# Expert tiles of layer 1: weight copies ahead of the row loads, smaller first units, and matmuls that keep TensorE occupied

## The chip, the cores and the metric

The kernel runs on one core of a Trainium2 chip. A core has five engines with instruction streams of their own: PE (TensorE, matmuls into PSUM), DVE (VectorE), ACT (ScalarE), POOL (GpSimd) and SP (SyncE, which here only issues DMAs). Each engine takes its instructions in order; between engines, order is kept by semaphores. The metric is the device time of one execution in microseconds (us), and a time of a kernel is the median over its runs.

## The reference

Two layers run one after the other over the same tokens, 8 sequences of 512 tokens with 128 channels. Each layer is an attention block (a recurrent scan) and a mixture of experts, both added to the residual. The change lies in the experts of layer 1:

```python
logits = hidden_states @ router_w + router_b
probs = jax.nn.softmax(logits, axis=-1)
topw, topi = jax.lax.top_k(probs, K)                    # K = 4 of E = 16 experts
topw = topw / jnp.sum(topw, axis=-1, keepdims=True)
combine = jnp.sum(jax.nn.one_hot(topi, E) * topw[..., None], axis=2)

def body(acc, expert):
    w1e, b1e, w2e, b2e, ce = expert                     # 128 x 256, 256, 256 x 128, 128
    hmid = jax.nn.gelu(x @ w1e + b1e, approximate=False)
    return (acc + (hmid @ w2e + b2e) * ce[:, None], None)
```

So of 4096 tokens each goes to 4 of 16 experts: 16384 rows of work, each through two matmuls of 128 x 256 with a Gelu between them.

## The kernel before

**Stages.** The program runs layer 0's attention, layer 0's experts, layer 1's attention with its router, then layer 1's experts. Each stage has its own pools of tiles on the chip; a pool that opens where an older one was closed takes over its addresses, and then the first write of a new tile waits for the last use of whatever lay there.

**Layer 1's router** (`route1`) ends each sequence by scattering its rows: for each token tile and each of its four experts, POOL issues one indirect DMA (line 1532, 128 of them) that writes 128 rows of 130 numbers (128 channels, the weight of the expert, and the row's place in the result) into a table in memory, `rows1`, which has one region per expert. The order of this stage is found by a small planner (`Order`), which hands out engines by estimated costs and ranks.

**Layer 1's experts** (from line 1584) are written out by hand, in the order given. Rows of one expert are cut into tiles of 128; since how many rows an expert gets is known only at run time, there are 144 tiles, enough for the worst case, in 36 quads of four.

- `plan()` (lines 1619 to 1677) counts the rows of each expert and works out, for every tile, its expert, where its rows start in `rows1`, and which rows are to be dropped. A last pair of passes, line 1672, spreads one of these lists over the partitions.
- `fetch(q)` loads the four row tiles of a quad into `de` (line 1690): three from SP's queue, one from ACT's. Four quads are asked for ahead. All these loads wait until the last row scatter has landed.
- `prepare(q)` transposes the four tiles on PE (line 1696). For each tile DVE copies the weights of its expert out of the resident tables `fw1` and `fw2` at an offset read from `off1` (lines 1680, 1701, 1702), and then the transposed rows out of PSUM (`dT`, line 1703).
- `first(q)` multiplies by the first weights (line 1712, eight matmuls of 128 x 128) and ACT applies Gelu with its bias (line 1718, eight activations).
- `second(q)` multiplies by the second weights (line 1729, eight matmuls). DVE works out the destinations (`to`, line 1736) and scales the results (`qy`, line 1737). POOL then scatters them, one indirect DMA for each tile (line 1739, 144 in all), into `res1`.
- `results(b)` at the end loads the four results of each token back (`yk`), and POOL and DVE add them to the residual (lines 1775 and 1777).

The loop calls `prepare(q + 1)`, `first(q)`, `fetch(q + 4)` and `second(q - 1)` in this order for each `q`, after one `prepare(0)` ahead of it. Buffers: the weight copies `qw1` and `qw2` have three and four, `dT` and `qh` three, `y` four; the PSUM banks `qT` and `qyp` are two each and `mid` four.

The pool of all these tiles, `work2`, opens where layer 1's attention had its `work1`, in which the row scatters' sources (`rows`) lie as well.

`fill` (line 952) is an older piece: the planner may put matmuls of `ident` by `zeros` into gaps of PE in the earlier stages. None is in the expert stage.

Of the kernel before, what the change touches and what calls it, by code (L numbers as in the profile page):

```python
# [9 lines left out]
F32 = mybir.dt.float32  # L10
I32 = mybir.dt.int32
# [3 lines left out]
ALU = mybir.AluOpType  # L15
AX = mybir.AxisListType

P = 128
B = 8
S = 512  # L20
NT = S // P
C = 128
# [167 lines left out]
def two_layers(ctx: ExitStack, tc: tile.TileContext, a: dict, out: bass.AP):  # L190
    nc = tc.nc

    const = ctx.enter_context(tc.tile_pool(name="const", bufs=1))
# [31 lines left out]
    ident = const.tile([P, P], F32, name="ident")  # L225
# [212 lines left out]
    def tiled(t2):  # L438
        return t2.rearrange("p (t c) -> p t c", t=NT)
# [593 lines left out]
        nc.scalar.preload_act_table_set(EXP)  # L1033

    stage.close()
    work = stage.enter_context(tc.tile_pool(name="work1", bufs=1))
    small = stage.enter_context(tc.tile_pool(name="small1", bufs=1))

# [2 lines left out]
    full = [P, NT, K1, E1]  # L1041
    ys_ring = ring(work, 2, [P, NT, 2, C], "ys")
    u_ring = ring(work, 4, tokens, "u")
    hn_ring = ring(work, 2, tokens, "hn")
    h1_ring = ring(work, 2, columns, "h1T")
    v_ring = ring(work, 3, columns, "vT")
    gk_ring = ring(work, 2, [ng, S], "gk")
    kq_ring = ring(work, 2, columns, "kq")
    za_ring = ring(work, 2, [ng, S], "za")
    gate_ring = ring(work, 3, columns, "gate")  # L1050

    four = [P, DK, S]
    kb_ring = ring(work, 3, four, "kb")
# [531 lines left out]
    fw1, fw2 = late  # L1585

    stage.close()
    work = ctx.enter_context(tc.tile_pool(name="work2", bufs=2))


    de_ring = ring_of(work, 8, [P, 4, W1], "de")
    to_ring = ring_of(work, 4, [P, 4], "to", I32)
    w1_ring = ring_of(work, 3, [P, 4, WE], "qw1")
    w2_ring = ring_of(work, 4, [P, 4, I1], "qw2")
    dT_ring = ring_of(work, 3, [P, S], "dT")
    hT_ring = ring_of(work, 3, [P, NC1, S], "qh")
    y_ring = ring_of(work, 4, [P, 4, C], "qy")
# [94 lines left out]
    def prepare(q):  # L1692

        ps = qT_banks[q % 2]
        for i in range(4):
            nc.tensor.transpose(ps[:, i * P : (i + 1) * P], de[q][:, i, 0:C], ident)  # L1696
        w1_q, w2_q, dT = w1_ring[q % 3], w2_ring[q % 4], dT_ring[q % 3]
        for i in range(4):
            n = 4 * q + i
            at = value(off1[0:1, n : n + 1], ET.DVE, 0, (E1 - 1) * WE)  # L1700
            nc.vector.tensor_copy(w1_q[:, i, :], fw1[:, bass.ds(at, WE)])  # L1701
            nc.vector.tensor_copy(w2_q[:, i, :], fw2[:, bass.ds(at, I1)])  # L1702
        nc.vector.tensor_copy(dT, ps)  # L1703

    def first(q):

        w1_q, dT, hT = w1_ring[q % 3], dT_ring[q % 3], hT_ring[q % 3]
        mid = mid_banks[2 * (q % 2) : 2 * (q % 2) + 2]
        for i in range(4):
            here = slice(i * P, (i + 1) * P)  # L1710
            for c in range(NC1):
                nc.tensor.matmul(  # L1712
                    mid[c][:, here], lhsT=w1_q[:, i, c * P : (c + 1) * P], rhs=dT[:, here], start=True, stop=True
                )
        for i in range(4):
# [6 lines left out]
    def second(q):  # L1722

        w2_q, hT, to, y = w2_ring[q % 4], hT_ring[q % 3], to_ring[q % 4], y_ring[q % 4]
        ps = qy_banks[q % 2]
        for i in range(4):
# [9 lines left out]
        nc.vector.tensor_tensor(to, de[q][:, :, DEST].bitcast(I32), nowhere[:, 4 * q : 4 * q + 4], ALU.max)  # L1736
        nc.vector.tensor_mul(y, tiled(ps), de[q][:, :, WEIGHT : WEIGHT + 1].to_broadcast([P, 4, C]))
        for i in range(4):
            nc.gpsimd.indirect_dma_start(  # L1739
                out=res1_w[4 * q + i],  # L1740
                out_offset=bass.IndirectOffsetOnAxis(ap=to[:, i : i + 1], axis=0),
                in_=y[:, i, :],
                in_offset=None,
                bounds_check=NA - 1,
                oob_is_err=False,
            )
# [71 lines left out]
```

## Time and profile before

| what | us |
|---|---|
| median of six runs | 1025.02 (1018.0 to 1028.74) |
| the profiled execution, whole time | 1025.66 |
| its span on the core | 1023.9 |
| PE busy, of the span | 794.2 |
| DVE busy | 629.3 |
| ACT busy | 472.6 |
| POOL busy | 467.2 |
| last row scatter of the router (line 1532) starts | 780.90 |
| first result scatter (line 1739) starts | 798.28 |
| last result scatter starts | 985.05 |

The span is counted from the first instruction on the core; the whole time has 1.76 us more around it. A row of the timeline gives the start, the duration, the engine, the line in the kernel, the operation, output and inputs, how many such instructions are merged, and in brackets how long the engine stood idle before it and what released it. A group's row gives the busy time, then the mean duration of one in nanoseconds, then the idle time before the group. PE's operations are f32 matmuls here, and the trace records each pass of one. The granted clock of PE is 1.0 or 0.5 of the full one, in steps of 3.41 us.

### The profile page before, as it was taken

What the parts mean: (1) busy time and instruction counts of PE and PEld (TensorE: products, weight loads), DVE (VectorE), ACT (ScalarE), POOL (GpSimd) and SP (SyncE); (2) the same over time, 40 slices, a digit from 0 to 9 for tenths busy, and PEclk for the clock granted to TensorE, in tenths of its full rate; (3) what the DMA queues carried; (4) which work ended last, traced back from release to release, by engine and by line L of the source; (5) the groups of instructions that cost most, each with busy time, mean ns of one, the idle gap of its engine ahead of it and who ended that gap; (6) DMA issues with size and microseconds to landing.
All of it is one profiled execution on the core that took longest, in us unless ns stands there. A gap on an engine that the chain in (4) does not pass through costs nothing. (4 is left out here: it accounts for less than half of the span.)

```text
span 1023.9 us, 13443 instructions
## 1 busy us (share of the span) xinstructions
PE 794.2 (78%) x3819; PEld 520.9 (51%) x3819; DVE 629.3 (61%) x1584; ACT 472.6 (46%) x1040; POOL 467.2 (46%) x474
## 2 busy tenths in 40 slices
PE   5978999899798939969678899787942998988400
PEld 3635466455363614423346555455621997877400
DVE  5496999788767301114678666767552777666317
ACT  6543665663352414418545686465620553434200
POOL 6200003232844434530000826878774677777753
PEclk9896789898787759989988997978865999999855
DMA  7994675566244330026992406765212443332138
GB/s 177 219 266 109 164 185 141 148 169 141 68 111 112 107 84 12 16 83 180 231 229 73 120 14 155 193 186 161 91 50 71 126 116 105 98 100 78 50 132 280
DMA packets 81675, 131.93 MB, mean 129 GB/s; under 512 B 13044, under 2 KB 58998, under 8 KB 74432
## 3 DMA queue, kind: packets, MB, share of 16 engines
q1 hardware_dynamic: 52544, 91.12, 34.9%
q0 software_dynamic: 14832, 27.84, 9.3%
q10 hardware_dynamic: 14224, 12.11, 3.9%
q8 instruction: 30, 0.49, 0.2%
q14 instruction: 45, 0.37, 0.1%
HBM read 94.79 MB, written 41.14 MB: 133 GB/s over the span
## 5 line engine op out<-in xcount | busy, mean ns | idle before, releaser
L1532 POOL DMA_INDIRECT rows<-rows,si x128 | 152.5, 1191 | 175.1 <-DVE tmp L1502 113.6
L876 POOL DMA_INDIRECT row<-rows,si x64 | 90.2, 1409 | 212.6 <-DVE qT L587 109.0
L1739 POOL DMA_INDIRECT res<-qy,to x144 | 143.7, 998 | 60.4 <-issue 31.2
L1718 ACT ACTIVATE qh<-mid,qw 128x128 f32<-128x128 f32 x288 | 79.3, 378 | 121.6 <-PE mid L1712 86.6
L1712 PE MATMUL mid<-dT,qw 128*128 128x128 f32 x576 | 75.1, 286 | 18.8 <-DVE dT L1703 18.8
L671 PE MATMUL acc<-add,center 128*128 128x512 f32 x128 | 78.4, 770 | 9.7 <-DVE add L700 8.0
L1712 PEld LDWEIGHTS mid<-dT,qw 128*128 128x128 f32 x576 | 70.0, 199 | 23.4 <-DVE dT L1703 23.2
L694 DVE TENSOR_TENSOR_SCAN add<-dec,add 128x2048 f32<-128x2048 f32 x16 | 70.8, 4425 | 0.7
L1729 PE MATMUL qyp<-qw,qh 128*128 128x128 f32 x576 | 70.0, 275 | 0.0
L1729 PEld LDWEIGHTS qyp<-qw,qh 128*128 128x128 f32 x576 | 67.2, 192 | 0.0
L179 ACT ACT_TABLE_LOAD x48 | 61.6, 1283 | 5.4 <-issue 3.5
L1701 DVE COPY qw<-fw 128x258 f32 x144 | 45.0, 313 | 29.8 <-DMA rows<-rows,si 16.6
L671 PEld LDWEIGHTS acc<-add,center 128*128 128x128 f32 x128 | 30.9, 252 | 54.5 <-issue 35.7
L1012 POOL DMA_INDIRECT res<-y,de x32 | 31.4, 982 | 45.3 <-DVE dT L985 20.7
L789 PE MATMUL bank<-xT,rw 128*128 128x512 f32 x64 | 41.7, 787 | 5.5 <-ACT xT L781 3.8
L1702 DVE COPY qw<-fw 128x256 f32 x144 | 43.7, 303 | 0.2 <-issue 0.2
L1317 PE MATMUL acc<-ident,kb 128*128 128x128 f32 x256 | 36.2, 309 | 9.2 <-DVE kb L1307 9.2
L1317 PEld LDWEIGHTS acc<-ident,kb 128*128 128x128 f32 x256 | 34.9, 223 | 13.1 <-DVE kb L1307 13.0
L1777 DVE TENSOR_TENSOR x<-x,yk 128x512 f32<-128x512 f32 x24 | 24.1, 1012 | 28.5 <-DMA yk<-res 27.4
L952 PE MATMUL idle_bank<-zeros,ident 128*128 128x512 f32 x76 | 40.6, 662 | 0.8 <-DVE y L1006 0.8
L662 ACT ACTIVATE dec<-dec 128x2048 f32<-128x2048 f32 x16 | 30.5, 1908 | 22.6 <-DVE dec L682 22.6
L1696 PE MATMUL qT<-ident,de 128*128 128x128 f32 x144 | 23.4, 282 | 21.2 <-DMA de<-rows 21.1
(337 smaller groups left out, 1757.5 us busy)
## 6 DMA issues: line engine op xcount, KB each, us to landing
add<-keys SPq DMA_DIRECT2D x16, 1024.0 KB
qb_first<-queries SPq DMA_DIRECT2D x8, 1024.0 KB
qb_second<-queries SPq DMA_DIRECT2D x8, 1024.0 KB
kb<-pairs SPq DMA_DIRECT2D x8, 1024.0 KB
gb_both<-decays SPq DMA_DIRECT2D x8, 1024.0 KB
qb_both<-pairs SPq DMA_DIRECT2D x8, 1024.0 KB
yk<-res SPq DMA_DIRECT2D x8, 1024.0 KB
de<-rows SPq DMA_DIRECT2D x108, 65.0 KB
```

The costliest lines, as they stand in the source:

```text
L179: self.load(table)
L671: nc.tensor.matmul(acc, lhsT=center, rhs=st[:, j, :], start=g + j == 0, stop=(g + 1) * J + j == D + J - 1)
L694: nc.vector.tensor_tensor_scan(flat, dec.rearrange("p j t -> p (j t)"), flat, 0.0, ALU.mult, ALU.add)
L876: nc.gpsimd.indirect_dma_start(out=row0_w[(b * NT + t) * 2 + k], out_offset=bass.IndirectOffsetOnAxis(ap=m.si[:, t, k : k + 1], axis=0), i ...
L1317: nc.tensor.matmul(chunk(acc, t), lhsT=chunk(st[:, j, :], t), rhs=ident, start=j + t == 0, stop=j + t == DK + NT - 2)
L1532: nc.gpsimd.indirect_dma_start(out=rows1_w[(b * NT + t) * K1 + k], out_offset=bass.IndirectOffsetOnAxis(ap=m.si[:, t, k : k + 1], axis=0), ...
L1701: nc.vector.tensor_copy(w1_q[:, i, :], fw1[:, bass.ds(at, WE)])
L1702: nc.vector.tensor_copy(w2_q[:, i, :], fw2[:, bass.ds(at, I1)])
L1712: nc.tensor.matmul(mid[c][:, here], lhsT=w1_q[:, i, c * P : (c + 1) * P], rhs=dT[:, here], start=True, stop=True)
L1718: nc.scalar.activation(hT[:, c, here], mid[c][:, here], AF.Gelu, bias=w1_q[:, i, I1 + c : I1 + c + 1])
L1729: nc.tensor.matmul(ps[:, here], lhsT=hT[:, c, here], rhs=w2_q[:, i, c * C : (c + 1) * C], start=c == 0, stop=c == NC1 - 1,)
L1739: nc.gpsimd.indirect_dma_start(out=res1_w[4 * q + i], out_offset=bass.IndirectOffsetOnAxis(ap=to[:, i : i + 1], axis=0), in_=y[:, i, :], i ...
```

## The change

Four things are done together.

- The tiles of layer 1's attention are split over two pools, `early1` and `work1`. The weight rings `qw1` and `qw2` of the expert stage get a pool of their own, `early2`, which takes the place of `early1`; the tiles with the row scatters' sources stay in `work1`, under `work2`.
- The weight copies leave `prepare` for a function `weights(q)`. It is called for quads 0, 1 and 2 right after `plan()`, before any row is fetched, and for the others two quads ahead.
- The loop runs over units. Quad 0 is four units of one tile, quad 1 two units of two tiles, all others one unit of four tiles. `dT`, `qh`, `to`, `y` and the PSUM banks rotate by unit, the weights by quad.
- After the weight copies, `warm(24)` puts 24 matmuls of `ident` by `zeros` (128 x 512) on PE, then one matmul of one column on a tile `gate` that POOL sets to zero, then five more.

```diff
     stage.close()
+    early_work = stage.enter_context(tc.tile_pool(name="early1", bufs=1))
     work = stage.enter_context(tc.tile_pool(name="work1", bufs=1))
...
-    hn_ring = ring(work, 2, tokens, "hn")
+    hn_ring = ring(early_work, 2, tokens, "hn")
...
     stage.close()
+    early_work = ctx.enter_context(tc.tile_pool(name="early2", bufs=1))
     work = ctx.enter_context(tc.tile_pool(name="work2", bufs=2))
...
-    w1_ring = ring_of(work, 3, [P, 4, WE], "qw1")
-    w2_ring = ring_of(work, 4, [P, 4, I1], "qw2")
+    w1_ring = ring_of(early_work, 3, [P, 4, WE], "qw1")
+    w2_ring = ring_of(early_work, 4, [P, 4, I1], "qw2")
...
+    def weights(q):
+
+        w1_q, w2_q = w1_ring[q % 3], w2_ring[q % 4]
         for i in range(4):
             n = 4 * q + i
             at = value(off1[0:1, n : n + 1], ET.DVE, 0, (E1 - 1) * WE)
             nc.vector.tensor_copy(w1_q[:, i, :], fw1[:, bass.ds(at, WE)])
             nc.vector.tensor_copy(w2_q[:, i, :], fw2[:, bass.ds(at, I1)])
...
+    units = [(0, range(i, i + 1)) for i in range(4)] + [(1, range(0, 2)), (1, range(2, 4))]
+    units += [(q, range(4)) for q in range(2, QUADS)]
...
+    def prepare(u):
+
+        q, tiles_of = units[u]
+        ps, dT = qT_banks[u % 2], dT_ring[u % 3]
+        for i in tiles_of:
+            nc.tensor.transpose(ps[:, i * P : (i + 1) * P], de[q][:, i, 0:C], ident)
+        nc.vector.tensor_copy(dT[:, span(tiles_of)], ps[:, span(tiles_of)])
...
+    def warm(n):
+
+        for _ in range(n):
+            nc.tensor.matmul(mid_banks[3], lhsT=ident, rhs=zeros, start=True, stop=True)
+
     AHEAD = 4
+    gate = const.tile([P, 1], F32, name="gate")
     with tc.manual_schedule():
         plan()
+        for q in range(3):
+            weights(q)
+        warm(24)
+        nc.gpsimd.memset(gate, 0.0)
+        nc.tensor.matmul(mid_banks[3][:, 0:1], lhsT=ident, rhs=gate, start=True, stop=True)
+        warm(5)
         for q in range(AHEAD):
             fetch(q)
-        prepare(0)
-        for q in range(QUADS + 1):
-            if q + 1 < QUADS:
-                prepare(q + 1)
-            if q < QUADS:
-                first(q)
-            if q + AHEAD < QUADS:
-                fetch(q + AHEAD)
-            if q > 0:
-                second(q - 1)
+        for u in range(len(units) + 1):
+            here = u < len(units)
+            q = units[u][0] if here else QUADS
+            if u < 5:
+                prepare(u)
+            if 4 < u + 1 < len(units) and u >= 4:
+                prepare(u + 1)
+            if here:
+                first(u)
+                if units[u][1][0] == 0 and q + AHEAD < QUADS:
+                    fetch(q + AHEAD)
+            if u > 0:
+                second(u - 1)
+            if here and units[u][1][-1] == 3 and 0 < q < QUADS - 2:
+                weights(q + 2)
```

The rings `h1T`, `vT`, `gk`, `kq`, `za` and `kb` move to `early1` like `hn`. `first` and `second` do for the tiles of a unit what they did for the four of a quad: the matmuls, activations, destinations, multiplies and scatters are the same in number for each tile, and DVE's `dT`, `to` and `qy` are one instruction for each unit.

More of the change, by code (lines that the diff above doesn't have):

```diff
@@ L1043, in two_layers @@
     u_ring = ring(work, 4, tokens, "u")
-    hn_ring = ring(work, 2, tokens, "hn")
[L1045 to L1049, printed above, removed]
+    hn_ring = ring(early_work, 2, tokens, "hn")
+    h1_ring = ring(early_work, 2, columns, "h1T")
+    v_ring = ring(early_work, 3, columns, "vT")
+    gk_ring = ring(early_work, 2, [ng, S], "gk")
+    kq_ring = ring(early_work, 2, columns, "kq")
+    za_ring = ring(early_work, 2, [ng, S], "za")
     gate_ring = ring(work, 3, columns, "gate")
     four = [P, DK, S]
-    kb_ring = ring(work, 3, four, "kb")
+    kb_ring = ring(early_work, 3, four, "kb")
     gb_both = experts.tile([P, 2, DK, S], F32, tag="first", name="gb_both")
@@ L1690, in fetch @@
                 queue.dma_start(de[q][:, i, :], rows1[bass.ds(at[i - tiles_of[0]], P), :])
[L1692 to L1697, printed above, removed]
+    def weights(q):
+        w1_q, w2_q = w1_ring[q % 3], w2_ring[q % 4]
         for i in range(4):
@@ L1702, in prepare, with span, first @@
             nc.vector.tensor_copy(w2_q[:, i, :], fw2[:, bass.ds(at, I1)])
[L1703 to L1709, printed above, removed]
+    units = [(0, range(i, i + 1)) for i in range(4)] + [(1, range(0, 2)), (1, range(2, 4))]
+    units += [(q, range(4)) for q in range(2, QUADS)]
+    def span(tiles_of):
+        return slice(tiles_of[0] * P, (tiles_of[-1] + 1) * P)
+    def prepare(u):
[4 more added lines that the diff above has]
+        nc.vector.tensor_copy(dT[:, span(tiles_of)], ps[:, span(tiles_of)])
+    def first(u):
+        q, tiles_of = units[u]
+        w1_q, dT, hT = w1_ring[q % 3], dT_ring[u % 3], hT_ring[u % 3]
+        mid = mid_banks[2 * (u % 2) : 2 * (u % 2) + 2]
+        for i in tiles_of:
             here = slice(i * P, (i + 1) * P)
@@ L1714, in first @@
                 )
-        for i in range(4):
+        for i in tiles_of:
             here = slice(i * P, (i + 1) * P)
@@ L1720, in first, with second @@
                 )
[L1722 to L1726, printed above, removed]
+    def second(u):
+        q, tiles_of = units[u]
+        w2_q, hT, to, y = w2_ring[q % 4], hT_ring[u % 3], to_ring[u % 4], y_ring[u % 4]
+        ps = qy_banks[u % 2]
+        for i in tiles_of:
             here = slice(i * P, (i + 1) * P)
@@ L1735, in second @@
                 )
-        nc.vector.tensor_tensor(to, de[q][:, :, DEST].bitcast(I32), nowhere[:, 4 * q : 4 * q + 4], ALU.max)
-        nc.vector.tensor_mul(y, tiled(ps), de[q][:, :, WEIGHT : WEIGHT + 1].to_broadcast([P, 4, C]))
-        for i in range(4):
+        of = slice(tiles_of[0], tiles_of[-1] + 1)
+        n = len(tiles_of)
+        nc.vector.tensor_tensor(
+            to[:, of], de[q][:, of, DEST].bitcast(I32), nowhere[:, 4 * q + of.start : 4 * q + of.stop], ALU.max
+        )
+        nc.vector.tensor_mul(
+            y[:, of, :],
+            ps[:, span(tiles_of)].rearrange("p (t c) -> p t c", c=C),
+            de[q][:, of, WEIGHT : WEIGHT + 1].to_broadcast([P, n, C]),
+        )
+        for i in tiles_of:
             nc.gpsimd.indirect_dma_start(
```

## The prediction

> **What bounds the kernel now.** I first read the chain that ended last, backwards from its end, then POOL's timeline over the stage that the change touches, then PE's and DVE's in the gap found there. The chain's last 38.85 us (last scatter at 985.05, span end 1023.9) are the loads and adds of `results`, which the change leaves alone. Before it, from 833 us on, nearly every link is a scatter of line 1739. POOL's timeline says why:
>
> ```profile
> 780.90 0.98 POOL L1532 DMA_INDIRECT rows<-rows,si  x1 [0.30 <-issue]
> 798.28 0.98 POOL L1739 DMA_INDIRECT res<-qy,to  x1 [16.40 <-DVE qw L1701]
> 799.57 1.01 POOL L1739 DMA_INDIRECT res<-qy,to  x1 [0.30 <-issue]
> 800.88 0.98 POOL L1739 DMA_INDIRECT res<-qy,to  x1 [0.30 <-issue]
> 802.17 1.10 POOL L1739 DMA_INDIRECT res<-qy,to  x1 [0.30 <-issue]
> ...
> 809.38 0.98 POOL L1739 DMA_INDIRECT res<-qy,to  x1 [0.30 <-DVE dT L1703]
> 810.66 1.07 POOL L1739 DMA_INDIRECT res<-qy,to  x1 [0.30 <-issue]
> ...
> 985.05 0.98 POOL L1739 DMA_INDIRECT res<-qy,to  x1 [0.30 <-issue]
> ```
>
> To be seen: after the last row scatter of the router POOL is idle for 16.40 us; from 798.28 on it issues 144 scatters at (985.05 - 798.28) / 143 = 1.306 us apart with hardly a hole. PE makes a quad in 4.01 us, POOL needs 4 x 1.306 = 5.22 us for it. So once the queue ahead of POOL is full, POOL alone sets the end, and the change is worth what it does to the start of the steady row of scatters. I follow the ninth scatter (quad 2's first), 809.38 now; behind it lie 985.05 - 809.38 = 175.7 us of scatters and the 38.85 us tail.
>
> PE's timeline in the gap, and fill matmuls of the same shape as the new ones elsewhere in it:
>
> ```profile
> 569.44 2.84 PE L952 MATMUL idle_bank<-zeros,ident 128*128 128x512 f32 x6
> ...
> 764.80 1.32 PE L1672 MATMUL qT<-used,ones 1*128 1x288 f32 x2 [0.54 <-DVE used L1668]
> 785.81 0.45 PE L1696 MATMUL qT<-ident,de 128*128 128x128 f32 x1 [19.68 <-DMA de<-rows]
> 786.95 0.47 PE L1696 MATMUL qT<-ident,de 128*128 128x128 f32 x1 [0.70 <-DMA de<-rows]
> 787.61 0.69 PE L1696 MATMUL qT<-ident,de 128*128 128x128 f32 x2 [0.18 <-DMA de<-rows]
> 788.85 1.43 PE L1696 MATMUL qT<-ident,de 128*128 128x128 f32 x4 [0.56 <-DMA de<-rows]
> 790.08 3.19 PE L1712 MATMUL mid<-dT,qw 128*128 128x128 f32 x16
> ```
>
> PE waits from 766 to 785.81 for rows, then works through the first quad at half clock. The groups give one more line:
>
> ```profile
> L952 PE MATMUL idle_bank<-zeros,ident 128*128 128x512 f32 x76 | 40.6, 662 | 0.8 <-DVE y L1006 0.8
> ```
>
> Its count has to be read with care: the program holds 38 such matmuls and the trace 76 records, so an f32 matmul is two passes. The six records of 2.84 us at 569.44 are three matmuls, and the starts of passes that follow each other stand 0.429 us apart at full clock and 0.853 at half. One fill matmul therefore costs **0.858 us** (1.706 at half clock), not 0.662.
>
> **The change, part by part.**
>
> *Weight copies ahead of the rows.* 24 copies (12 tiles, two each, about 0.66 us a tile with the register load between, by the rows at 783.77 to 786.3) move from behind the row scatters to right after `plan()`, 767.2 to about 775. Their new pool lets them: in the built program their first copy waits for loads of `fw1` (issued by 717.2), no longer for row scatters. Before, DVE did the first eight while the row loads flew, so the move takes 0 to 2.7 us (one quad's copies, 788.94 to 791.06 and the dT behind them) off the start. I put nothing in for it alone, since the new PE path below replaces the old one. Beside them POOL issues some seven row scatters. A scatter beside such copies took 1.07 to 1.10 us instead of 0.98, so the last rows come up to 7 x 0.12 = 0.8 us later, or at best not at all; 0 in my sum, because PE is then still in its fill; 0.8 if that cover is gone.
>
> The Trainium skill speaks against this step: "SBUF — State Buffer", in "SBUF: two separate sides" and the section after it, says that an f32 copy of VectorE locks GpSimd out of descriptor writing, and that a GpSimd DMA of 620 ns took 3100 ns beside one. By that, seven scatters would lose up to 7 x 2.5 = 17 us and the kernel some 10 us. The 1.10 us here, with copies beside, is against a loss of that size.
>
> *The gate.* In the source the memset of `gate` stands behind all row scatters. In the built program it stands on POOL among the set-up loads, ahead even of layer 0's scatters, since nothing orders it. So the matmul on `gate` waits for nothing, and no work on POOL moves. Cost: one matmul of 1 column, two weight loads of 0.19 us (the row of line 952's loads), 0.1 to 0.4; I take 0.3.
>
> *The fill.* 24 + 5 matmuls stand on PE ahead of `prepare(0)`, in order, with nothing to end them early. They start when the passes of line 1672 have streamed: 764.80 + 2 x 288 columns at half clock, 0.96, so 765.8. Half clock rules there (0.50 in 766 to 783). How soon does it rise? Before its rises PE had been dense for 2.9 us (376.73 to 379.65), 3.8 (788.85 to 792.66) and up to 7. I take a rise 3.0 us into the fill, 768.8; it may come between 768 and 771.8. In those 3.0 us 1.76 matmuls are done, the other 22.24 take 19.08, the gate 0.3, the last five 4.29: PE is free at **p = 792.4** (791.4 to 794.3). The rows have long landed: the transposes of quad 1 ran at 788.85. So `prepare(0)` goes back from 785.81 to 792.4, 6.6 us.
>
> Here a rule and the rows differ most. "TensorE: Matmul & The Clock Gate", "Back-to-back issue gap", gives 216 ns for a 512-column matmul at full clock. By it the fill would be over near 773, far ahead of the rows, and the sum would be that of the first rival below. The rows' two passes of 0.429 us decide for me.
>
> *Small units.* Quad 0 goes tile by tile, quad 1 in pairs. From p to the end of `second(6)`, quad 2's, PE must issue, at full clock: transposes of quads 0 to 4, 20 x 0.109 = 2.2; `first` of quads 0 to 3, 4 x 16 x 0.112 = 7.1; `second` of quads 0 to 2, 3 x 1.79 = 5.4; together 14.7. Units 0 to 4 also stall: transpose latency 0.28, the copy of one tile 0.26 (0.69 for four tiles, 0.27 for a 128-column read of PSUM, line 1135) or 0.40 for a pair, two hops of 0.05, less what overlaps: 0.6 each, 3.0 in all (0.4 to 0.9 each, so 2.0 to 4.5). In `first(0)` and later, ACT's two activations (0.65) hide behind the next tile's transpose, copy and `first`. Then the last pass drains 0.2, the multiply takes 0.69, POOL starts 0.28 after it (798.0 to 798.28): p + 14.7 + 3.0 + 1.17 = p + 18.9.
>
> The first scatter is earlier: transpose 0.28, copy, `first` 0.6, activations, transpose and `first` of tile 1 queued ahead of it, `second` 0.6 and a small multiply make 3.3 us, so about 795.7 against 798.28. But the next ones come 1.7 us apart, not 1.3, and quads 1 and 2 at PE's pace: the fifth at about 803.7 (803.58 before), the ninth at 792.4 + 18.9 = **811.3** against 809.38. That is **1.9 us later**. From there quad 3 is ready at 815.0 and POOL gets to it at 816.5, so POOL is the bound again and keeps its 1.306.
>
> *What else moves.* `fetch(0..3)` is issued by the same queues at the same waits; the row loads do not change. `weights(3)`, on DVE between quad 1's and quad 3's work, takes 2.4 us ahead of unit 7's dT; PE is in `first(6)` and `second(5)` then (2.7 us), so it is hidden, and 0.5 if not. The copies of `y` and `to` use four buffers each as before. In layer 1's attention the new pool shifts addresses; in the built program the order of work is the same but for one iota of POOL that moves ahead of layer 0's result scatters with waits that are long met: 0.
>
> **Sum.** The profiled execution took 1025.66 us (span 1023.9 and 1.76 around it). It becomes 1027.6. It lies 0.6 above the median of the six runs shown, 1025.02, so I forecast a median of **1026.9**, +0.2%. What a measurement of this kernel can tell from no change is about 0.5%, 5.1 us.
>
> **Rivals.**
>
> *PE is free when the rows land.* If a fill matmul cost 0.6 us or less, or the gate held PE only to the last row scatter with a fill that ended by then, p would be about 786.4 at full clock: ninth scatter at 786.4 + 18.9 = 805.3, 4.1 us earlier, so 1020.9. For it: the mean of 662 ns in the group's row, 24 x 0.662 = 15.9, just the 766 to 782 of the gap. Against it: the pass count. It decides from p below 790.5, where the ninth scatter is no later than before. Even then the gain stays under 0.5%, because PE's 14.7 us bind after a first scatter at 790.
>
> *Slower: the fill runs longer at half clock.* Each further 3.41 us window at half costs 3.41 / 2 = 1.7 us on p. It decides from p = 795.6, two windows more than I take: ninth scatter 814.5, time 1030.1 or above (all of the fill at half: 29 x 1.706 = 49.5 us, p = 815.6, and 1050). For it: the clock fell for one window inside dense work at 867.76. Against it: where PE's passes filled a 3.41 us window at half clock, the next was at full clock, with one exception (near 90 us).
>
> *The bubble closes as meant.* Ninth scatter as far ahead as the first could be, at full tile-by-tile pace: 9 us earlier, 1016. It would need PE to spend 5 us less from p on than its passes take; nothing in the profile speaks for it.
>
> **How the numbers follow.** Forecast, 1026.0 to 1028.9 by p and with the stalls' ends 1024.9 to 1030.4: 0.64. PE free with the rows: 0.12, within 0.5% unless other terms help, so a third of it counts as faster. Longer half clock: 0.12. The bubble closed: 0.04. The rest, 0.08, is what a median of a few runs that spread from 1018.0 to 1028.74 may add, to both sides. Range 1020.5 to 1031.5: it takes in the first rival and the beginning of the second. Faster by over 0.5%: 0.11; within: 0.72; slower: 0.17.
>
> **What would show it.** In the profile after: 58 records of the fill line from about 765.8 to 792 on PE without a gap, 0.429 apart after the first few; the first transpose of rows behind them, not behind a DMA; weight copies at 767 to 776; the first scatter near 795.7 but the ninth at 810 to 813; scatters 1.306 apart from there. Wrong would be a first transpose at 786 to 788, row scatters stretched well past 785, or scatters with holes after the ninth.

## The result and the profile after

The changed kernel takes 1032.41 us (median of 30 runs, 1025.01 to 1040.14) against 1026.33 us for the kernel before (67 runs): a ratio of 1.0064, 95% interval 1.0049 to 1.008. That is 6.6 us (5.0 to 8.2) slower. Forecast were 0.2% slower and 1026.9 us; the time lies 5.5 us above that and 0.9 us above the range. Of the 5.5 us, 1.3 are the yardstick: the forecast stood on the six runs shown (median 1025.02), and 67 runs of the same kernel have 1026.33.

The profiled execution reached the changed stage 3.9 us earlier than that of before (last row scatter of the router at 776.98 instead of 780.90), for reasons that lie ahead of it. So I count everything in this stage from the **start of the last row scatter** and write +x us. POOL's timeline of the changed kernel (start, duration, engine and line, what it does, in brackets the idle time before it and what ended that):

```profile
776.98 0.98 POOL L1533 DMA_INDIRECT rows<-rows,si  x1 [0.30 <-issue]
793.39 0.98 POOL L1762 DMA_INDIRECT res<-qy,to  x1 [15.42 <-DVE to L1753]
797.44 0.98 POOL L1762 DMA_INDIRECT res<-qy,to  x1 [3.07 <-DVE to L1753]
800.10 0.98 POOL L1762 DMA_INDIRECT res<-qy,to  x1 [1.67 <-DVE qy L1756]
802.64 0.98 POOL L1762 DMA_INDIRECT res<-qy,to  x1 [1.57 <-DVE qy L1756]
805.00 0.98 POOL L1762 DMA_INDIRECT res<-qy,to  x1 [1.38 <-DVE qy L1756]
808.09 1.09 POOL L1762 DMA_INDIRECT res<-qy,to  x1 [2.10 <-issue]
...
812.61 0.98 POOL L1762 DMA_INDIRECT res<-qy,to  x1 [0.78 <-DVE qw L1700]
...
988.52 0.98 POOL L1762 DMA_INDIRECT res<-qy,to  x1 [0.30 <-issue]
```

The first scatter comes at +16.41 (before: +17.38), a gain of 1 us. But holes of 1.4 to 3.1 us follow, and the ninth comes at 812.61 - 776.98 = **+35.63**; before, it came at 809.38 - 780.90 = **+28.48**. That is 7.15 us later, close to the 6.6 of the times; for other kernels below the two differ by up to 5 us. Behind the ninth the row runs as before: 175.91 us to the last scatter (before 175.67) and 39.5 us of tail (before 38.85). Within these two executions the parts add up: -3.9 us ahead of the stage, +7.15 to the ninth scatter, +0.2 in the row and +0.6 in the tail make the 4.1 us between their spans (1028.0 and 1023.9).

PE's timeline over the same stretch:

```profile
761.81 1.32 PE L1674 MATMUL qT<-used,ones 1*128 1x288 f32 x2 [0.54 <-DVE used L1670]
763.06 22.35 PE L1774 MATMUL mid<-zeros,ident 128*128 128x512 f32 x48
785.25 0.28 PE L1784 MATMUL mid<-gate,ident 128*128 128x1 f32 x2
785.39 4.54 PE L1774 MATMUL mid<-zeros,ident 128*128 128x512 f32 x10
789.76 0.27 PE L1715 MATMUL qT<-ident,de 128*128 128x128 f32 x1
```

The fill is 58 passes without a gap, and the gate's matmul waits for nothing. The first transpose of rows stands behind the last fill pass, at 789.76 = +12.78. It waits for no DMA, because its rows have long been there: without a fill this transpose starts at +4.9, as soon as they land (785.81 - 780.90 in the kernel before).

ACT's timeline (ACTq is its DMA queue):

```profile
790.95 0.62 ACT L1732 ACTIVATE qh<-mid,qw 128x128 f32<-128x128 f32 x2 [36.20 <-PE mid L1726]
795.25 0.38 ACTq L1692 DMA_DIRECT2D de<-rows  x1
795.67 1.14 ACT L1732 ACTIVATE qh<-mid,qw 128x128 f32<-128x128 f32 x4 [4.10 <-DMA de<-rows]
```

This I had not forecast. After the first unit's two activations ACT stands still for 4.10 us. Its next instruction is the load of quad 4's fourth tile, which `fetch(4)` puts there. That load waits for a DMA completion semaphore, one of eight that the row loads of SP and of ACT use in turn in this trace, and the use of it before this one is a load of quad **5**, which SP issued at 793.29 and which landed at 795.23; ACT's load goes out at 795.25. In the kernel before, the same load (793.81) waited for a load of quad 1, issued at 787.07 and long landed. The activations of the second unit stand behind it, and PE waits for them (2.02 us idle up to 796.09, in front of the products of line 1744); its granted clock falls to 0.60 in the 4 us from 797, with 0.98 before and 1.00 behind.

### The profile page after: what moved, and what is told of

Its sections match the earlier page's. It is cut to its first block, busy times and chain, and to the rows that moved or that the text cites. A ratio compares the mean times of both kernels' runs of the same rounds, so it can differ in the third digit from the quotient of the medians.

```text
span 1028.0 us, 13557 instructions
## 1 busy us (share of the span) xinstructions
PE 810.5 (79%) x3879; PEld 528.0 (51%) x3879; DVE 631.9 (61%) x1596; ACT 472.7 (46%) x1040; POOL 471.2 (46%) x475
## 5 line engine op out<-in xcount | busy, mean ns | idle before, releaser
L876 POOL DMA_INDIRECT row<-rows,si x64 | 94.3, 1474 | 207.1 <-DVE qT L587 110.8
L1762 POOL DMA_INDIRECT res<-qy,to x144 | 143.8, 999 | 67.7 <-issue 32.6
L671 PE MATMUL acc<-add,center 128*128 128x512 f32 x128 | 75.9, 747 | 10.3 <-DVE add L700 6.3
L1726 PEld LDWEIGHTS mid<-dT,qw 128*128 128x128 f32 x576 | 67.8, 192 | 26.7 <-DVE dT L1716 26.7
L789 PE MATMUL bank<-xT,rw 128*128 128x512 f32 x64 | 37.4, 714 | 5.3 <-ACT xT L781 3.6
L1136 DVE BATCH_NORM_STATS2 st<-acc 128x6 f32<-128x128 f32 x64 | 17.5, 273 | 32.6 <-PE acc L1162 24.2
```

What stands on the lines that cost most here:

```text
L671: nc.tensor.matmul(acc, lhsT=center, rhs=st[:, j, :], start=g + j == 0, stop=(g + 1) * J + j == D + J - 1)
L876: nc.gpsimd.indirect_dma_start(out=row0_w[(b * NT + t) * 2 + k], out_offset=bass.IndirectOffsetOnAxis(ap=m.si[:, t, k : k + 1], axis=0), i ...
L1726: nc.tensor.matmul(mid[c][:, here], lhsT=w1_q[:, i, c * P : (c + 1) * P], rhs=dT[:, here], start=True, stop=True)
L1762: nc.gpsimd.indirect_dma_start(out=res1_w[4 * q + i], out_offset=bass.IndirectOffsetOnAxis(ap=to[:, i : i + 1], axis=0), in_=y[:, i, :], i ...
```

## Experiments

Three suspects: **T1**, the fill holds PE 8 us past the rows' arrival. **T2**, the stall of ACT. **T3**, the small units themselves. The yardstick is the ninth scatter; every kernel was also timed against the kernel before on its own chip. None of them leaves out any of the reference's work. The runs e1 to e9 ran on two chips where the kernel before takes 1027.7 us (1027.69 and 1027.64); the changed kernel's row is that of the result above:

| kernel | PE's first transpose of rows | first scatter | ninth | ninth against before | time against before, 95% interval |
|---|---|---|---|---|---|
| before | +4.9 | +17.38 | +28.48 | | |
| changed | +12.78 | +16.41 | +35.63 | +7.15 | 1.0064 (1.0049 to 1.008) |
| e1: no fill | +4.92 | +10.25 | +26.04 | -2.4 | 1.0000 (0.9972 to 1.0027) |
| e2: ACT issues no load from quad 4 on | +13.39 | +17.01 | +32.80 | +4.3 | 1.0068 (1.0038 to 1.0098) |
| e5: before + early weight copies | +5.1 | +17.91 | +28.95 | +0.5 | 1.0007 (0.998 to 1.0034) |
| e6: before + fill | +11.80 | +20.76 | +31.80 | +3.3 | 1.006 (1.0032 to 1.0087) |
| e4: e2 with 19 fill matmuls | +5.04 | +8.69 | +24.48 | -4.0 | 0.9974 (0.995 to 0.9999) |
| e7: e1, transposes ahead | +5.1 | +9.42 | +23.42 | -5.1 | 0.9998 (0.997 to 1.0026) |
| e8: e4, transposes ahead | +5.2 | +8.72 | +23.45 | -5.0 | 0.9975 (0.9942 to 1.0009) |
| e9: e4, whole quads | +5.2 | +17.25 | +28.29 | -0.2 | 1.0029 (0.9996 to 1.0062) |

One profile stands behind each ninth scatter, and 12 runs behind each time (30 for the changed kernel), so a time is good to about 3 us. Five of the nine times lie 2.4 to 3.2 us above what the ninth scatter says and e7's 4.9; those of the changed kernel, e5 and e4 lie -0.6, +0.2 and +1.3 from it. That difference is not explained. The ninth scatter leaves out two stretches that move as well: in these ten executions the last row scatter started between 776.98 and 789.82 us, and the tail took 38.85 to 39.93. One profile can't tell how much of the first belongs to a kernel. The moved pools of layer 1's attention are not the reason, for e6 is without them (2.9 us above) and e5 has them (0.2).

**e1, no fill.** The lines `warm(24)`, the memset, the matmul on `gate` and `warm(5)` are taken out:

```diff
-        warm(24)
-        nc.gpsimd.memset(gate, 0.0)
-        nc.tensor.matmul(mid_banks[3][:, 0:1], lhsT=ident, rhs=gate, start=True, stop=True)
-        warm(5)
```

> The changed kernel without its 29 fill matmuls and the gate. The measure is the start of the ninth result scatter counted from the start of the last row scatter: 28.5 us in the kernel before, 35.6 in the changed one. In the built program the scalar queue's load for quad 4 then waits for a load of quad 1, long landed, as in the kernel before, so the stall of the activations should be gone too. Fill and stall both real: PE starts at about +5 at half clock, ninth at 5 + 18.9 + 3 = about +27, so 8 us under the changed kernel and 1 to 2 under the kernel before (ratio to before about 0.998). Only the stall matters: 4 us under the changed kernel, 3 above before. The small units themselves are what costs: ninth above +30, still 2 us or more slower than before.

PE's timeline without the fill:

```profile
788.21 0.45 PE L1715 MATMUL qT<-ident,de 128*128 128x128 f32 x1 [18.77 <-DMA de<-rows]
789.04 1.22 PE L1726 MATMUL mid<-dT,qw 128*128 128x128 f32 x4 [0.38 <-DVE dT L1716]
```

Now the transpose waits for its rows again, and the ninth scatter comes 9.6 us sooner than in the changed kernel, at +26.04. The loss is gone: 1.0000 (expected about +27 and 0.998). So the other parts of the change together neither cost nor bring a time that can be measured, which speaks against T3 as the cause. The run does not part T1 from T2, because without the fill ACT's load waits for a load of quad 1 again (issued at 789.97, ACT's at 791.89).

**e2, no load on ACT's queue from quad 4 on.**

```diff
-        for engine, queue, tiles_of in ((ET.SP, nc.sync, range(3)), (ET.Activation, nc.scalar, range(3, 4))):
+        both = ((ET.SP, nc.sync, range(3)), (ET.Activation, nc.scalar, range(3, 4)))
+        for engine, queue, tiles_of in both if q < AHEAD else ((ET.SP, nc.sync, range(4)),):
```

> The changed kernel, but from quad 4 on all four row loads of a quad are issued by SP and none by the scalar queue; fill and small units stay. Theory that the scalar queue's load of quad 4 holds up the activations: the 4.10 us gap in front of the second unit's activations goes, ninth scatter from +35.6 to about +31.7, 4 us faster than the changed kernel, some 2 to 3 us (0.3%) slower than before. Theory that the fill alone is late: no change against the changed kernel, ninth at +35.6, because some other wait takes the place of that gap.

ACT's timeline:

```profile
794.27 0.62 ACT L1733 ACTIVATE qh<-mid,qw 128x128 f32<-128x128 f32 x2 [37.44 <-PE mid L1727]
795.47 0.63 ACT L1733 ACTIVATE qh<-mid,qw 128x128 f32<-128x128 f32 x2 [0.58 <-PE mid L1727]
797.21 0.63 ACT L1733 ACTIVATE qh<-mid,qw 128x128 f32<-128x128 f32 x2 [1.11 <-PE mid L1727]
```

```profile
779.70 0.98 POOL L1533 DMA_INDIRECT rows<-rows,si  x1 [0.30 <-issue]
812.50 0.98 POOL L1763 DMA_INDIRECT res<-qy,to  x1 [0.78 <-DVE qw L1701]
```

The stall is gone: 0.58 us in front of the second unit instead of 4.10. From PE's first transpose to the ninth scatter it takes 32.80 - 13.39 = 19.4 us, in the changed kernel 35.63 - 12.78 = 22.85. So the stall is worth 3.4 us in the profile. Of that 2.8 us arrives at the ninth scatter, since this execution's fill ended 0.6 us later against the rows. The ninth scatter was expected at +31.7 and the time 0.3% above the kernel before. The time shows none of the gain: 1.0068. Less 2.8 us, the changed kernel's 1.0064 would be 1.0037, just outside this interval (1.0038 to 1.0098), but the 1.0064 has an interval of its own (1.0049 to 1.008). What the stall costs in time is left open by this run; that it is the whole loss (a time of 1.000) lies outside the interval.

**e6, the kernel before with the fill alone** (`warm`, the gate and the four lines of the fill behind `plan()`, nothing else).

> The kernel before with the fill and the gate alone. In the built program the fill alone already moves the scalar queue's load of quad 4 behind loads of quad 5, as in the changed kernel; but with a whole quad the activations ahead of it end at about +18.4, when those loads have landed, so no gap of more than 0.5 us is to be seen there. PE free at +12.8, quads at full clock: ninth at 12.8 + 17 to 20 = +29.8 to +32.8, 1.3 to 4.3 us slower than before. If instead the load stalls whole quads as well: +34 or more.

```profile
789.74 4.54 PE L1751 MATMUL mid<-zeros,ident 128*128 128x512 f32 x10
794.11 1.04 PE L1696 MATMUL qT<-ident,de 128*128 128x128 f32 x8
```

```profile
782.31 0.98 POOL L1532 DMA_INDIRECT rows<-rows,si  x1 [0.30 <-issue]
814.11 0.98 POOL L1739 DMA_INDIRECT res<-qy,to  x1 [0.30 <-issue]
```

PE's eight transposes of quads 0 and 1 all stand behind the fill, at +11.80. The ninth scatter is at +31.80, inside the expected stretch, and the time is 1.006: in time **the fill alone loses what the whole change loses**, though its ninth scatter is only 3.3 us late and not 7.15. Two expectations missed. The time, 6.2 us (3.3 to 8.9), was expected at 1.3 to 4.3. And the gap in ACT is there with whole quads as well:

```profile
797.36 2.17 ACT L1718 ACTIVATE qh<-mid,qw 128x128 f32<-128x128 f32 x8 [37.88 <-DVE qw L1701]
801.83 0.34 ACTq L1690 DMA_DIRECT2D de<-rows  x1
802.28 0.88 ACT L1718 ACTIVATE qh<-mid,qw 128x128 f32<-128x128 f32 x3 [2.75 <-PE qT L1696]
```

The load again goes out late (+19.5), and the activations behind it start 2.75 us after the first quad's (the view ends at 803). The semaphore that it waits for was last used by a load of quad 5 (798.50), as in the changed kernel. So the fill brings the stall with it; why the build then hands out the semaphores in another order is not shown. POOL's row does not show this stall: from the first scatter to the ninth it takes 11.04 us, in the kernel before 11.10. So what e6 loses in this stage is the fill's late end.

**e5, the early weight copies alone** (the changed kernel's pools and `weights`, without fill, in units of whole quads).

> The early weight copies and their own pool alone: no fill, and quads 0 and 1 go as whole quads as in the kernel before. If the early copies help by what stood in the path (2.7 us of copies before the first products): first scatter about +14.7 instead of +17.4, ninth +25.8 to +28.5, 0 to 2.7 us faster than before. If the copies beside the last row scatters hold those up as the Trainium skill's page on SBUF says: row scatters further apart than 1.4 us and 5 us or more slower.

No gain: first scatter +17.91, ninth +28.95, time 1.0007. The copies are out of the way, but whole quads wait for something else (see e9). No loss either. In the changed kernel, as here, the 24 copies run beside six row scatters:

```profile
769.10 0.98 POOL L1533 DMA_INDIRECT rows<-rows,si  x1 [0.30 <-issue]
770.39 0.98 POOL L1533 DMA_INDIRECT rows<-rows,si  x1 [0.31 <-issue]
771.68 0.98 POOL L1533 DMA_INDIRECT rows<-rows,si  x1 [0.30 <-issue]
```

These are lines of the changed kernel: 0.98 us long and 1.29 apart, as the later ones without copies (775.70 and 776.98); all six take 0.98 to 1.02 us, in e5 0.98 to 1.04. The Trainium skill, "SBUF — State Buffer", section "SBUF: two separate sides" and the one after it, says that f32 copies of VectorE lock GpSimd out of descriptor writing. In these runs that cost is not to be seen.

**e4, a fill that ends with the rows' arrival** (e2 with `warm(14)` in place of `warm(24)`, so 19 matmuls).

> The changed kernel with a fill of 19 matmuls (14 and 5) in place of 29, and the loads of quads 4 on issued by SP alone. The fill then ends at 13.4 - 10 x 0.858 = about +4.8 after the last row scatter, when the first rows land (+4.9). If what the changed kernel loses is PE's late start, the ninth result scatter goes from +32.8 (29 matmuls, same loads) to 5 + 19.4 = +24.4, 8 us faster than that and 4 us (0.4%) faster than the kernel before. If a warm PE is worth nothing because the small units are a chain of waits: +26.0 as without any fill, and no difference to the kernel before.

```profile
789.00 4.54 PE L1775 MATMUL mid<-zeros,ident 128*128 128x512 f32 x10
793.92 0.30 PE L1716 MATMUL qT<-ident,de 128*128 128x128 f32 x1 [0.38 <-DMA de<-rows]
```

```profile
788.88 0.98 POOL L1533 DMA_INDIRECT rows<-rows,si  x1 [0.30 <-issue]
813.36 0.98 POOL L1763 DMA_INDIRECT res<-qy,to  x1 [0.78 <-DVE qw L1701]
```

Now the fill ends and the transpose waits 0.38 us for its rows. Ninth scatter +24.48, forecast +24.4. Against e2, which differs in ten fill matmuls alone, that is 8.3 us earlier (10 x 0.858 = 8.6), and the times are 1.0068 and 0.9974, 9.6 us apart, with intervals that do not meet. From PE's first transpose to the ninth scatter both take 19.4 us, so within the stage they differ by PE's start alone. That is **T1, shown**. It is, with e8, also the best version: 2.7 us (0.1 to 5.1) faster than before on this chip, which is barely clear of no gain.

**e9, the same with whole quads.**

> Early weight copies and the fill of 19 matmuls, loads of quads 4 on by SP, but whole quads from the start as in the kernel before. With the full fill in the kernel before, quads took 20.0 us from PE's first transpose to the ninth scatter and 8.95 to the first. With PE free at +5 and no copies of weights between: first scatter about +13.5, ninth +24 to +25, 3.5 to 4.5 us (0.4%) faster than the kernel before. If small units are what brings the gain: it stays at +27 or more.

A miss that explains e5. PE's timeline:

```profile
792.77 0.30 PE L1715 MATMUL qT<-ident,de 128*128 128x128 f32 x1 [0.43 <-DMA de<-rows]
...
794.76 0.44 PE L1715 MATMUL qT<-ident,de 128*128 128x128 f32 x2 [1.04 <-DMA de<-rows]
795.62 1.38 PE L1715 MATMUL qT<-ident,de 128*128 128x128 f32 x4 [0.42 <-DMA de<-rows]
796.79 3.01 PE L1726 MATMUL mid<-dT,qw 128*128 128x128 f32 x16
```

With whole quads, quad 1's four transposes stand ahead of quad 0's products, and they wait for quad 1's rows (795.62, 1.38 us long, with waits inside). The last row scatter was at 787.56, so the products start at +9.2, just as without fill and with a cold clock (790.08 - 780.90 = +9.2 in the kernel before). The first scatter of whole quads comes at +17.4, +17.9 and +17.25 in the three kernels that have no late fill: its start hangs on the rows, not on the weights. What a full clock would bring there stays open, because the fill did not keep it up. PE stood idle between the transposes, the granted clock was 0.50 from 795.6 to 799.0, and the products took 3.01 us, near the 3.19 of the kernel before; the next quad's, at full clock, take 1.95. The small units are what brings it to +8.7, because unit 0 needs one tile's rows.

**e7 and e8, transposes of the next unit always ahead** (e1 and e4 with the order of the kernel before for all units).

```diff
-            if u < 5:
-                prepare(u)
-            if 4 < u + 1 < len(units) and u >= 4:
+            if u == 0:
+                prepare(0)
+            if u + 1 < len(units):
                 prepare(u + 1)
```

> The changed kernel without fill and gate, and with the transposes and the copy to dT of the next unit always ahead of the products of this one, as the kernel before had it with whole quads; the changed kernel does that only from the fifth unit on. Without the fill the tiles' scatters stood 1.74, 1.74, 2.34, 2.36, 3.09 us apart, and with a warm PE just the same, so I take it that waits inside a unit (transpose, copy, product, activation) and not PE's passes set that pace. If so: tiles closer to 1.3 to 1.6 us, ninth scatter from +26.0 to about +23 to +24.5, 2 us faster. If PE's passes at half clock set it: +26 as before.

> Both: fill of 19 matmuls, loads of quads 4 on by SP, and the next unit's transposes always ahead. If waits inside the units and a cold clock are what keeps the small units from paying: first scatter about +8.7, PE's 14.7 us of passes from +5 set the ninth, 5 + 14.7 + 1.2 + 0.5 = +21.4, 7 us (0.7%) faster than the kernel before. If the rows land one after another too slowly for it (loads 0.5 us apart, quads 1.5 us): +24 or more, no better than one of the two edits alone.

e7's ninth scatter is at +23.42 as expected, but its time is 0.9998: no gain that can be measured, and its row of the table is the one where ninth and time disagree most. In e8 the first four tiles come 1.29 us apart (+8.72, 10.00, 11.29, 12.58), as close as POOL goes, so waits inside the units did set the 1.74. But its ninth misses +21.4 by 2 us, and e8's PE shows where most of them go:

```profile
803.67 0.33 PE L1716 MATMUL qT<-ident,de 128*128 128x128 f32 x1
804.38 0.33 PE L1716 MATMUL qT<-ident,de 128*128 128x128 f32 x1 [0.38 <-DMA de<-rows]
805.07 0.44 PE L1716 MATMUL qT<-ident,de 128*128 128x128 f32 x2 [0.36 <-DMA de<-rows]
805.34 1.95 PE L1727 MATMUL mid<-dT,qw 128*128 128x128 f32 x16
```

These are quad 3's transposes. They wait for quad 3's rows, ahead of quad 2's products (805.34): the same trap one stage on. They hold PE for 1.67 us where four transposes without waits take 0.43, so this is 1.2 of the 2 us. Time 0.9975, as e4.

**Other chips.** The last ten runs were to weigh the stall by time and to try another order. They fell on chips on which every kernel takes about 10% longer (the kernel before 1120 to 1128 us), and there the stage has another rhythm.

> The kernel before, profiled once more, to see how far the measure itself moves from execution to execution. If the measure is good: ninth scatter 28.5 after the last row scatter within 0.7 us. If the kernel before varies with the clock: up to +31.

> The changed kernel once more, as it is, beside its version without the scalar queue's loads on the same chip. The stall of the activations is a matter of the built program, so it should be there again: 4 us in front of the second unit's activations, first transpose of rows at +12 to +13.5 (the clock's rise moves the fill's end by up to 1.7 us), ninth scatter +35 to +36.5; 1.006 of the kernel before.

> The changed kernel with the loads of quads 4 on by SP alone, once more. The first profile had its ninth scatter at +32.8, 2.8 us ahead of the changed kernel's, but the times did not show it (1.0068 of before against 1.0064). Theory that the stall costs what the profile shows: ninth within 1 us of +32.5 and a time 2 to 3.5 us below the changed kernel's on this chip, 1.003 to 1.004. Theory that the fill's late end is all that matters for the time: no more than 1 us below it, 1.006.

> The changed kernel as it is, beside the next three on one chip. Stall of about 4 us in front of the second unit's activations, ninth scatter 35 to 36.5 us after the last row scatter, 1.006 of the kernel before.

> The changed kernel with the loads from quad 4 on by SP alone. If the stall costs in time what the profile shows: no stall, ninth scatter +32 to +33, time 2 to 3.5 us under the changed kernel on this chip. If the late end of the fill is all that counts: no more than 1 us under it.

> The changed kernel as it is. On a chip where the stage runs as in the first profiles: 4 us of stall, ninth scatter 35 to 36.5 us after the last row scatter, 1.006 of the kernel before.

> The changed kernel with the loads from quad 4 on by SP alone. If the stall costs in time what the profile shows: ninth scatter +32 to +33 and 2 to 3.5 us under the changed kernel of the same call. If only the fill's late end counts: no more than 1 us under it.

The changed kernel took 1.0116 (1.0066 to 1.0166), 1.0047 (1.001 to 1.0083) and 1.0125 (1.0075 to 1.0174) of the kernel before; without ACT's loads it took 1.0105 (1.0054 to 1.0156), 1.0069 (1.0037 to 1.0101) and 1.0095 (1.006 to 1.0131). PE and POOL of the changed kernel there, second of the three:

```profile
825.92 1.32 PE L1674 MATMUL qT<-used,ones 1*128 1x288 f32 x2 [0.54 <-issue]
827.17 23.02 PE L1774 MATMUL mid<-zeros,ident 128*128 128x512 f32 x48
...
850.17 4.54 PE L1774 MATMUL mid<-zeros,ident 128*128 128x512 f32 x10
854.54 0.27 PE L1715 MATMUL qT<-ident,de 128*128 128x128 f32 x1
```

```profile
834.51 1.06 POOL L1533 DMA_INDIRECT rows<-rows,si  x1 [0.30 <-issue]
858.17 0.98 POOL L1762 DMA_INDIRECT res<-qy,to  x1 [22.60 <-DVE to L1753]
```

`plan()`'s last matmul stands 8.6 us ahead of the last row scatter there (6.5 to 8.6 in the profiles on these chips), not 15.2. The fill takes the same 27 us from where it starts, and PE is free at 854.54 - 834.51 = +20.0. The ninth scatter of the three comes at +40.3 to +41.1 (+32.0 in the kernel before, whose yardstick so moved by 3.5 us with the chip; I had allowed 2.5). What the stalled load waited for is long done by then (SP's load of quad 5 at 850.78, ACT's load at 856.44), and in front of the second unit ACT idles 0.58 us with or without that load. So these six runs can't tell what the stall costs. Its share in the time stays open. What they show is that nothing ties the fill to the rows.

The order "products, next transposes, second products" (`prepare(u + 1)` behind `first(u)`, with 19 fill matmuls and no ACT loads), and quad 2 in pairs on top of it:

> Fill of 19 matmuls, loads of quads 4 on by SP, and from the start the order: products of this unit, then the transposes of the next, then the second products of the one before. With the next unit's transposes always first, quad 2's products stood behind transposes that waited for quad 3's rows, and the ninth scatter came 3.0 us after the eighth; in the new order a unit's products wait for its own rows alone. If that is so: tiles 1.3 us apart up to the fourth, no hole in front of the ninth beyond 1.5 us, ninth scatter +21.5 to +22.5, 6 us (0.6%) faster than the kernel before. If the ninth stays at +23.4 or later, something else than the order holds it.

> Fill of 19 matmuls, loads from quad 4 on by SP, and the order: products of this unit, transposes of the next, second products of the one before. If transposes waiting for later rows held the ninth scatter at +23.4: tiles 1.3 us apart, ninth at +21.5 to +22.5, 6 us (0.6%) faster than the kernel before. If not: +23.4 or later, 0.25% faster as with the order before.

> The same as the one before it, and quad 2 goes in pairs too, so that its first two tiles need not wait for its last two. If the size of the units holds the ninth scatter: 1 to 1.5 us earlier than with quad 2 as a whole, +20.5 to +21. If the rows or POOL's own row hold it: no difference within 0.5 us.

On these chips even 19 matmuls end at +11.7, where the kernel before, in its one profile on such a chip, has its first rows at +5.5. The new order, timed on two chips, took 1.0107 (1.0046 to 1.0168) on the first; on the second there is no ratio, its median is 1128.47 us against 1120.55. With pairs the time was 1.0097 (1.0066 to 1.0127). On the second chip the ninth scatters were at +32.6 with the new order and +30.3 with pairs. Both miss the expectations, and not by the late fill alone: the rows were there, and still the first four tiles came 1.29, 1.38 and 2.70 us apart, not 1.3, and from PE's first transpose to the ninth scatter the new order took 20.9 us, against 20.4 in the changed kernel and 18.6 with pairs. So there the new order gained nothing, and pairs brought the ninth scatter 2.3 us forward without a better time. A fill that is right on one chip is about 6 us too long on another, and none of the versions run there was shown to be faster than the kernel before. The two orders remain untested where their rows come in time.

## Why the prediction was wrong

Within the profile the mechanism was right: POOL's steady row sets the end, the ninth scatter carries the change, the fill outlasts the wait for the rows, and a gain at the first scatter is lost by the ninth. The sum was short: 1.9 us forecast, 7.15 in the profile, 6.6 in the times. Term by term, against the last row scatter:

- **The fill's length, right.** 26.6 us forecast, 763.06 to 789.76 = 26.7 measured; passes 0.429 us apart at full clock. "TensorE: Matmul & The Clock Gate" of the Trainium skill, "Back-to-back issue gap", gives 216 ns for a 512-column matmul; by that the fill would have been over some 7 us after its start, by the prediction's estimate. The trace decides: two passes for each f32 matmul, 26.7 us.
- **PE free at p, 1.3 us short.** "PE is free at **p = 792.4**" is +11.5; it was +12.78. The fill began at -13.9, not at -15.1: `plan()`'s last matmul stood 15.2 us ahead of the last row scatter in this execution, 16.1 in that of the kernel before, and the first pass followed it by 1.25 us, not 1.0. The 3.0 us at half clock that I took are what the changed kernel had. In e2 the granted clock rose only 6.2 us into the fill, which made it 28.3 us long.
- **Small units from p, within 0.5.** "p + 18.9" was 19.4 in e2 and e4, where ACT does not stall.
- **The stall, left out: the step that failed, as far as the profile tells.** "*What else moves.* `fetch(0..3)` is issued by the same queues at the same waits; the row loads do not change." is true of those four, and the step stops there. `fetch(4)` now stands behind the first unit's two activations instead of a quad's eight, on ACT's queue, and its wait had changed to a load of quad 5. I costed ACT at nothing ("hide behind the next tile's transpose, copy and `first`"), and that cover was gone: 3.4 us in the profile.

1.9 + 1.3 + 0.5 + 3.4 = 7.1. So of the 5.2 us by which the sum was short at the ninth scatter, the stall is 3.4. For the time this is not shown: e2, without the stall, is no faster (1.0068). The sum also took a shift of the ninth scatter as the same shift of the time, and e2 took 7.0 us more than before where its ninth scatter is 4.3 us late; this part is not explained. That the fill's late end makes most of the loss in time is shown (e6, and e4 against e2). It stood in the sum as 6.6 us of PE's start, against which the small units were to win most back; without the fill they win nothing that the times show (e1, 1.0000).

**Early weights at 0** held (e5), for the better reason that whole quads wait for rows. **The gate** waited for nothing, as forecast. **The first scatter** was forecast at 795.7, +14.8, and came at +16.41, 1.6 later, 1.3 of it from p. **Row scatters** were not slowed. The rival **"PE is free when the rows land"** gave 4.1 us less than before; e4, which makes it true, has its ninth scatter 4.0 us earlier and takes 2.7 us less. Of the rival **"the bubble closes as meant"** e4 shows how far it goes: its first scatter is 8.7 us earlier than before's and its ninth 4.0. The rival **"the fill runs longer at half clock"** happened in part, as e2's 6.2 us show, but it was not needed. Its "one exception" holds only for steps full of wide passes: in the profile of the kernel before, steps in which PE was busy throughout, but mostly with narrow passes or with passes on part of the array (from 82.7, 509.4 and 669.8 us), were followed by another at half clock. No step full of 128 x 512 passes, like those of the fill, was.

## What to carry to other kernels

A fill of fixed length in front of a wait is only worth its end: count its passes (two for f32), set them against the slack from the trace, and expect the slack to move with the chip; 19 matmuls gained 0.26%, barely clear of noise, where 29 lost 0.64%, and both were too long on another chip. When work is cut into smaller units, go through every instruction that now stands between two units on each engine's queue, DMA issues included, and look up in the built program what each of them waits for now. If an early start brings nothing, look for work on later data that is queued in front of the first unit's own: the transposes of quad 1 held quad 0, whatever was done for the weights.

## What was not expected of the hardware

- A DMA issued from ACT's queue can wait for a load issued on SP's queue for a later quad, because the two queues take their completion semaphores from one set in turn (eight in this trace). Here SP's load landed at 795.23 and ACT's went out at 795.25. It held up 4.10 us of activations that needed neither. An edit on PE alone (e6) changed which load it waits for.
- POOL's row has a hole of 2.10 us in front of the sixth result scatter in every kernel with small units, with nothing that the profile shows to wait for (`808.09`, `<-issue`); with whole quads on the first two chips it is 0.8 us. On the slower chips holes of 2 to 3 us stood all along the row, which took 1.6 us a scatter instead of 1.31. What they are is open. The ninth scatter of the changed kernel has idle time of its own ahead of it (0.78 us, up to a release by DVE), so the hole is not what sets it.
- The clock's rise under dense passes took 2.9 to 6.2 us from the fill's first pass in executions of nearly the same code. In all 15 profiles with a fill it came at the end of a 3.41 us step of the granted clock: of the first step if the fill had 2.90 us or more of it (2.90 in e6, 3.02 in the changed kernel), of the next one if it had less (2.80 in e2, 2.73 in e4). So where in a step the fill starts moved its end by up to 1.6 us.
